# A three-layer CIN kernel: preparation on four array tiles, two blocks by turns at the start, and a tail by quarters

## The chip, the cores and the metric

The kernel runs on one core of a Trainium2 chip. The metric is device time in microseconds (us) of one execution; a median of several runs is given. The profile is one profiled execution, whose span is counted from the first to the last instruction. The engines are called PE (TensorE, the matrix engine), PEld (its weight loads), DVE (VectorE), ACT (ScalarE), POOL (GpSimd) and SP (SyncE). All arithmetic is in fp32.

## The reference

B = 1024 samples have F = 39 fields of E = 64 numbers each. Three layers of a compressed interaction network multiply every feature map with every field and mix the products; each layer is summed over E, and one linear form makes a number of the sums.

```python
def _cin_layer(Xk, X0, W, b):
    O = W.shape[0]
    Hk, Fdim = (Xk.shape[1], X0.shape[1])
    Wr = W.reshape(O, Hk, Fdim)
    return jnp.einsum('bhe,bfe,ohf->boe', Xk, X0, Wr) + b[None, :, None]

X0 = sparse_embedding            # (1024, 39, 64)
Xk = X0
outs = []
for W, b in ((W0, b0), (W1, b1), (W2, b2)):   # (64, 39*39), (64, 64*39), (64, 64*39)
    Xk = _cin_layer(Xk, X0, W, b)
    outs.append(Xk.sum(axis=-1))
cin_output = jnp.concatenate(outs, axis=-1)
return cin_output @ fc_w.T + fc_b             # (1024, 1)
```

The kernels use that all layers but the first are linear in the last feature map. fc's third part times W2 gives a small matrix v2 (64 x 39, with fc's second part as column 40). v2 times W1 gives, for every pair of fields, 64 weights beside the 64 of W0. These 128 weights for each pair of fields (a 41st "field" of ones takes in linear terms) are the table of 1600 rows. Products of fields are formed once for each unordered pair, so that the weights of (a, b) and (b, a) are fetched from the table and added (wa + wb).

## The kernel before

The batch is cut into 32 blocks of 32 samples (2048 columns of sample times E). A block's fields lie in DRAM (xd, two blocks in a table, with a row of ones each). For every block, GpSimd gathers rows into four tiles of 128 partitions, r[n][:, 0..3], so that the six products of two tiles cover nearly all pairs of fields; what is left, half a chunk to a block, is the product of u and v for two blocks at once.

```python
PAIRS = ((0, 1), (0, 2), (0, 3), (1, 2), (2, 3), (1, 3))
NPAIR = len(PAIRS)          # 6
NCHUNK = NPAIR + 1          # 7
MM, SUB, BLK = 512, 1024, 2048
prods = ctx.enter_context(tc.tile_pool(name="prods", bufs=4))
psum = ctx.enter_context(tc.tile_pool(name="psum", bufs=4, space=PSUM))   # tiles of 128 x 1024
...
def gather_rows(dst, n, k):                      # L117
    table = xd[n // 2 % NTAB][: FT if k < 4 else 2 * FT]
    nc.gpsimd.indirect_dma_start(
        dst, None, table, bass.IndirectOffsetOnAxis(ap=lists[:, k : k + 1], axis=0)
    )
def roll(n, tiles=range(4)):
    r[n] = rt[n % 2]
    for i in tiles:
        gather_rows(r[n][:, i], n, n % 2 * 4 + i)
def roll_half(n):
    gather_rows(ut[n // 2 % 2], n, 8)
    gather_rows(vt[n // 2 % 2], n, 9)
```

The preparation loads the weights, forms v2, then the table in DRAM, and fetches the weights of each chunk from it by gathers (cut):

```python
nc.sync.dma_start(w2s, w2.rearrange("o (s n) -> (o s) n", s=2))
for k in range(2):
    nc.scalar.dma_start(fc2[k:128:2, k : k + 1], fcv[:, 2:3])
nc.scalar.dma_start(fc, fcv)
nc.scalar.dma_start(w1s, w1)
load(0, nc.gpsimd)
nc.gpsimd.memset(ones, 1.0)
nc.gpsimd.dma_start(xd[0][F : 2 * FT : FT], ones)
nc.gpsimd.dma_start(tablev[0:F, 0:F, H : 2 * H], w0t)
... # lists of rows, on DVE
roll(0, (0, 1, 2))
for t4 in range(4):                               # v2 = fc . W2
    nc.tensor.matmul(pv[32 * t4 : 32 * t4 + 32, 0:n8], fc2, w2s[:, t4 * n8 : (t4 + 1) * n8], ...)
nc.vector.tensor_copy(vrow, pv[:, 0:n8])
for k in range(2):
    nc.sync.dma_start(v2[32 * k : 32 * k + 32, 0:F], vrow[k:128:32])
...
for g in range(5):                                # v2 . W1, L273
    nc.tensor.matmul(pt[g // 2][at : at + FT, :n], v2, w1v[:, f0:f1, :], start=True, stop=True)
for g in range(5):                                # copies, and into the table
    ...
    engine.dma_start(tablev[:, f0:f1, 0:H], dst.rearrange("b (a h) -> b a h", h=H))
... # ones of the other tables, biases, load(1)
weights(0)
roll(0, (3,))
weights(1)
weights(2)
roll_half(0)
weights(3)
roll(1, (0, 1))
weights(4)
roll(1, (2, 3))
weights(5)
weights(6)
load(2)
load(3)
```

The main loop runs over steps (block, chunk); a product on DVE is four steps ahead of its matmuls, and a block's result is read out after the first step of the next one (cut):

```python
def product(n, c):                                # L324: DVE, 128 x 2048
    i, k = PAIRS[c]
    nc.vector.tensor_tensor(p, r[n][:, i], r[n][:, k], ALU.mult)
def multiply(n, c, p):                            # L341; L352 for the half chunk
    for m in range(BLK // MM):
        nc.tensor.matmul(po[n][m // 2][:, bass.ts(m % 2, MM)], wa[:, c, :], p[:, bass.ts(m, MM)], ...)
def finish(n):
    for h in range(BLK // SUB):                   # L372: ACT, 64 x 1024
        nc.scalar.activation(t, po[n][h][H:128, :], AF.Identity, bias=b0s[H:128])
    for h in range(BLK // SUB):                   # L376, L380: DVE
        nc.vector.scalar_tensor_tensor(gt[0:H], po[n][h][0:H, :], fc[:, 0:1], x1[h], ALU.add, ALU.mult)
        nc.vector.tensor_reduce(sums[:, b_at : b_at + SB], gt.rearrange("p (b e) -> p b e", e=E), AX.X, ALU.add)

steps = []
for n in range(0, NBLK, 2):
    steps += [(n, c) for c in range(NCHUNK)] + [(n + 1, c) for c in range(NPAIR)]
for at, (n, c) in enumerate(steps):
    ...                                           # gathers and loads for later blocks; wa += wb in the first block
    multiply(n, c, p.pop((n, c)))
    if c == 0:
        if n > 0:
            finish(n - 1)
        fields(n)
    if at + AHEAD < len(steps):
        p[steps[at + AHEAD]] = product(*steps[at + AHEAD])
finish(NBLK - 1)
last_weights()
for m in range(B // MM):                          # L427, L428
    nc.tensor.matmul(py[0:1, 0:MM], wfin, sums[:, bass.ts(m, MM)], start=True, stop=True)
    nc.scalar.activation(y[:, bass.ts(m, MM)], py[0:1, 0:MM], AF.Identity, bias=kfin)
nc.sync.dma_start(out.rearrange("b o -> o b"), y)
```

Of the kernel before, what the change touches and what calls it, by code (L numbers as in the profile page):

```python
# [51 lines left out]
F32 = mybir.dt.float32  # L52
I32 = mybir.dt.int32
AF = mybir.ActivationFunctionType
ALU = mybir.AluOpType
# [13 lines left out]
NPAIR = len(PAIRS)  # L69
NCHUNK = NPAIR + 1  # L70
MM = 512
SUB = 1024
BLK = 2048
BB = BLK // E
# [18 lines left out]
def cin_kernel(ctx: ExitStack, tc: tile.TileContext, x, w0t, b0, w1, b1, w2, b2, fc_w, fc_b, out):  # L93
# [7 lines left out]
    psum = ctx.enter_context(tc.tile_pool(name="psum", bufs=4, space=PSUM))  # L101
# [3 lines left out]
    r = {}  # L105
    xd = [dram.tile([2 * FT, BLK], F32, name=f"xd{k}") for k in range(NTAB)]

# [13 lines left out]
    def roll(n, tiles=range(4)):  # L121
        r[n] = rt[n % 2]
        for i in tiles:
            gather_rows(r[n][:, i], n, n % 2 * 4 + i)
# [8 lines left out]
    v2 = const.tile([H, FT], F32, name="v2")  # L133
# [16 lines left out]
    with prep as prep:  # L150
        w2s = prep.tile([128, FH // 2], F32, name="w2s")
        w1s = prep.tile([H, FH], F32, name="w1s")
        fc2 = prep.tile([128, 32], F32, name="fc2")
        ones = prep.tile([2, BLK], F32, name="ones")
        zeros = prep.tile([FT, 2 * H], F32, name="zeros")
# [4 lines left out]
        nc.gpsimd.iota(place, pattern=[[0, 1]], base=0, channel_multiplier=1)  # L160
        nc.vector.memset(fc2, 0.0)
        nc.vector.memset(zeros, 0.0)
        nc.vector.memset(warm, 0.0)
        nc.sync.dma_start(w2s, w2.rearrange("o (s n) -> (o s) n", s=2))
        fcv = fc_w.rearrange("o (l h) -> h (o l)", h=H)
        for k in range(2):
            nc.scalar.dma_start(fc2[k:128:2, k : k + 1], fcv[:, 2:3])
        nc.scalar.dma_start(fc, fcv)
        nc.scalar.dma_start(w1s, w1)
        nc.scalar.copy(warm, warm)  # L170
        load(0, nc.gpsimd)
        nc.gpsimd.memset(ones, 1.0)
        nc.gpsimd.dma_start(xd[0][F : 2 * FT : FT], ones)
        nc.gpsimd.dma_start(tablev[0:F, 0:F, H : 2 * H], w0t)
        nc.gpsimd.dma_start(tablev[:, F, :], zeros)
        nc.gpsimd.dma_start(tablev[F, 0:F, H : 2 * H], zeros[0:F, 0:H])
# [37 lines left out]
        fused(field[0], t, extra, field[0], ALU.mult, ALU.add)  # L214

# [9 lines left out]
        nc.vector.tensor_copy(lists[:, 0:4], fields_of[:, 0:4])  # L225
        nc.vector.tensor_scalar(lists[:, 4:8], fields_of[:, 0:4], float(FT), None, ALU.add)
        nc.vector.tensor_scalar(half, half, float(FT), None, ALU.mult)
        nc.vector.tensor_scalar(lists[:, 8:10], fields_of[:, 4:6], half, None, ALU.add)
        roll(0, (0, 1, 2))


        n8 = 8 * F
        pv = psum.tile([128, SUB], F32, name="pv", tag="po")
        vrow = prep.tile([128, n8], F32, name="vrow")
        for t4 in range(4):
            nc.tensor.matmul(  # L236
                pv[32 * t4 : 32 * t4 + 32, 0:n8],
                fc2,
                w2s[:, t4 * n8 : (t4 + 1) * n8],
                start=True,  # L240
                stop=True,
            )
        nc.vector.tensor_copy(vrow, pv[:, 0:n8])
        nc.vector.tensor_copy(v2[:, F:FT], fc[:, 1:2])
        for k in range(2):
            nc.sync.dma_start(v2[32 * k : 32 * k + 32, 0:F], vrow[k:128:32])
# [20 lines left out]
        part = prep.tile([128, 3, MM], F32, name="part")  # L267
        pt = [psum.tile([128, SUB], F32, name="pt", tag="po") for _ in range(3)]
        for g in range(5):
            f0, f1 = 8 * g, min(8 * g + 8, F)  # L270
            n = (f1 - f0) * H
            at = g % 2 * H
            nc.tensor.matmul(  # L273
                pt[g // 2][at : at + FT, :n], v2, w1v[:, f0:f1, :], start=True, stop=True
            )
        for g in range(5):
            f0, f1 = 8 * g, min(8 * g + 8, F)
            n = (f1 - f0) * H
            at = g % 2 * H
            src, dst = pt[g // 2][at : at + FT, :n], part[at : at + FT, g // 2, :n]  # L280
            if g % 2:
                nc.scalar.copy(dst, src)
            else:
                nc.vector.tensor_copy(dst, src)  # L284
            engine = nc.scalar if g % 2 else nc.sync
            engine.dma_start(tablev[:, f0:f1, 0:H], dst.rearrange("b (a h) -> b a h", h=H))
        for k in range(1, NTAB):
            nc.scalar.dma_start(xd[k][F : 2 * FT : FT], ones)
        for k, t in enumerate((b1, b2)):
            nc.scalar.dma_start(bias[:, k : k + 1], t.rearrange("(h o) -> h o", o=1))  # L290
        nc.scalar.dma_start(b0s[H:128], b0.rearrange("(h o) -> h o", o=1))
        nc.scalar.dma_start(fcb, fc_b.rearrange("(p o) -> p o", o=1))
        load(1)
# [7 lines left out]

    weights(0)
    roll(0, (3,))
    weights(1)
    weights(2)
    roll_half(0)
    weights(3)
    roll(1, (0, 1))
    weights(4)
    roll(1, (2, 3))  # L310
    weights(5)
    weights(6)
    load(2)
# [6 lines left out]
    def product(n, c):  # L320
        p = prods.tile([128, BLK], F32, name="p", tag="p")
        if c < NPAIR:
            i, k = PAIRS[c]
            nc.vector.tensor_tensor(p, r[n][:, i], r[n][:, k], ALU.mult)  # L324
        else:
            nc.vector.tensor_tensor(p, ut[n // 2 % 2], vt[n // 2 % 2], ALU.mult)  # L326
        return p

    def accumulators(n):
        po[n] = [psum.tile([128, SUB], F32, name="po", tag="po") for _ in range(BLK // SUB)]  # L330

    def multiply(n, c, p):
        first = n % 2 == 0
        if c == 0 and first:
            accumulators(n)
        if c == NPAIR:
            accumulators(n + 1)
        for m in range(BLK // MM):
            at = bass.ts(m % 2, MM)
            if c < NPAIR:  # L340
                nc.tensor.matmul(  # L341
                    po[n][m // 2][:, at],
                    wa[:, c, :],
                    p[:, bass.ts(m, MM)],
                    start=(c == 0 and first),
                    stop=(c == NPAIR - 1 and not first),
                )
                continue

            for h in range(2):  # L350
                w = slice(h * HR, (h + 1) * HR)
                nc.tensor.matmul(  # L352
                    po[n + h][m // 2][:, at],
                    wa[w, c, :],
                    p[w, bass.ts(m, MM)],
                    start=(h == 1),
                    stop=(h == 0),
                )
# [9 lines left out]
    def finish(n):  # L368
        x1 = []
        for h in range(BLK // SUB):  # L370
            t = work.tile([H, SUB], F32, name="x1", tag="x1")
            nc.scalar.activation(t, po[n][h][H:128, :], AF.Identity, bias=b0s[H:128])  # L372
            x1.append(t)
        for h in range(BLK // SUB):
            gt = g[n][h]
            nc.vector.scalar_tensor_tensor(  # L376
                gt[0:H], po[n][h][0:H, :], fc[:, 0:1], x1[h], ALU.add, ALU.mult
            )
            b_at = n * BB + h * SB
            nc.vector.tensor_reduce(  # L380
                sums[:, b_at : b_at + SB], gt.rearrange("p (b e) -> p b e", e=E), AX.X, ALU.add
            )

    def last_weights():

        pc = psum.tile([128, SUB], F32, name="pc", tag="po")
        nc.tensor.matmul(pc[0:F, 0:1], v2[:, 0:F], bias[:, 0:1], start=True, stop=True)
        nc.tensor.matmul(pc[0:1, MM : MM + 1], bias[:, 0:1], fc[:, 1:2], start=True, stop=False)
        nc.tensor.matmul(pc[0:1, MM : MM + 1], bias[:, 1:2], fc[:, 2:3], start=False, stop=True)
        nc.vector.memset(wfin[0:H], 1.0)  # L390
        nc.scalar.copy(wfin[H : H + F], pc[0:F, 0:1])
        nc.scalar.activation(kfin, pc[0:1, MM : MM + 1], AF.Identity, bias=fcb, scale=float(E))

    AHEAD = 4
    steps = []
    for n in range(0, NBLK, 2):
        steps += [(n, c) for c in range(NCHUNK)] + [(n + 1, c) for c in range(NPAIR)]
    p = {s: product(*s) for s in steps[:2]}
    for at, (n, c) in enumerate(steps):
        if c == 0:  # L400
            if 0 < n < NBLK - 1:
                roll(n + 1)
                if n % 2:
                    roll_half(n + 1)
            if n + 4 < NBLK:
                load(n + 4)
        if at == 0:
            for k in range(3):
                nc.vector.tensor_tensor(wa[:, k], wa[:, k], wb[:, k], ALU.add)  # L409
                if k < 2:  # L410
                    p[steps[2 + k]] = product(*steps[2 + k])
        elif n == 0 and c + 2 < NCHUNK:
            nc.vector.tensor_tensor(wa[:, c + 2], wa[:, c + 2], wb[:, c + 2], ALU.add)  # L413
        multiply(n, c, p.pop((n, c)))
        if c == 0:
            if n > 0:
                finish(n - 1)
            fields(n)
# [53 lines left out]
```

## Time and profile before

| | us |
|---|---|
| median of 3 runs | 780.49 (777.31 to 780.69) |
| profiled run, its span | 777.1, 775.1 |
| first product matmul starts | 33.3 |
| last product matmul ends | 761.9 |
| VectorE busy | 633.2 (82%) |
| GpSimd busy | 279.2 (36%) |

A line of a group of instructions is read: line of the program, engine, operation, output and input by name, sizes, how many, then busy us and mean ns of one, then the engine's idle time just ahead of them and what ended it. An fp32 matmul leaves two records. The chain of waits follows the work that ended last back to its beginning, so that its pieces add up to the span. A timeline line gives start, duration, engine, line and operation, and in brackets how long the engine was idle before.

### The profile page before, as it was taken

The page shows a single profiled execution, that of the slowest core. Times are in us where ns is not written, and L with a number is a line of the kernel's source. Part 1 is how long each engine was busy: PE and PEld are TensorE (multiplying, and loading weights), DVE is VectorE, ACT ScalarE, POOL GpSimd, SP SyncE. Part 2 cuts the span into 40 slices and gives each one's busy share as a digit, 9 for nine tenths or more (in the row PEclk, how much of TensorE's full clock was granted, in tenths as well). Part 3 has the DMA queues.
Part 4 walks back from the last instruction along what each step waited for, and adds up shares of the span by engine and source line. Part 5 has one row for each costly group of instructions (what it writes and reads, how often), then busy time and mean ns, then how long its engine had stood idle before and what let it go on. Part 6 is the DMA issues. An engine that isn't in the chain of part 4 may idle for free.

```text
span 775.1 us, 4926 instructions
## 1 busy us (share of the span) xinstructions
PE 735.6 (95%) x1820; PEld 316.8 (41%) x1820; DVE 633.2 (82%) x409; ACT 142.2 (18%) x136; POOL 279.2 (36%) x185
## 2 busy tenths in 40 slices
PE   3279999999999999999999999999999999999996
PEld 0134444444444444444444444444444444444442
DVE  4358888889888888988888898888888888889882
ACT  1012212122221212222121222212112221111222
POOL 4487343422334343223434322343432234343000
PEclk9999999999999999999999999999999999999998
DMA  7888875656776565676756567675656757545200
GB/s 202 258 321 318 334 291 217 222 220 233 321 249 276 213 231 213 228 315 249 288 214 224 218 231 301 250 296 219 219 222 227 292 217 309 216 195 214 96 0 0
DMA packets 65480, 181.40 MB, mean 234 GB/s; under 512 B 44345, under 2 KB 44385, under 8 KB 44907
## 3 DMA queue, kind: packets, MB, share of 16 engines
q0 software_dynamic: 23840, 169.46, 56.0%
q1 hardware_dynamic: 40259, 10.79, 6.1%
q10 hardware_dynamic: 1358, 0.84, 0.5%
q8 instruction: 14, 0.23, 0.1%
q14 instruction: 9, 0.07, 0.0%
HBM read 180.58 MB, written 11.10 MB: 247 GB/s over the span
## 4 chain that ended last, share of the span: by engine, by line
PE 92%; DMA 3%; POOL 2%; DVE 2%; issue 1%; ACT 0%; SPq 0%; POOLq 0%; DVEq 0%; ACTq 0%
PE po L341 83%; PE po L352 8%; DMA r<-xd,lists 1%; DMA table<-part 1%; POOL wa L298 1%; DMA v<-vrow 1%; DMA wb<-table,wlists 1%; POOL r L117 1%; PE pt L273 1%; PE py L427 0%; POOL wb L298 0%; DVE g L376 0%; DVE sums L380 0%; DMA bias<-in_b 0%; DVE fields_of L196 0%
## 5 line engine op out<-in xcount | busy, mean ns | idle before, releaser
L341 PE MATMUL po<-p,wa 128*128 128x512 f32 x1536 | 667.8, 596 | 19.3 <-DVE wa L409 15.1
L324 DVE TENSOR_TENSOR p<-r 128x2048 f32<-128x2048 f32 x192 | 435.9, 2291 | 96.9 <-PE po L341 68.3
L341 PEld LDWEIGHTS po<-p,wa 128*128 128x128 f32 x1536 | 291.5, 191 | 395.3 <-issue 383.6
L117 POOL DMA_INDIRECT r<-xd,lists x128 | 211.3, 1651 | 410.5 <-DVE p L324 384.0
L372 ACT ACTIVATE x<-po,b0s 64x1024 f32<-64x1024 f32 x64 | 71.1, 1111 | 427.1 <-PE po L352 244.6
L365 ACT COPY g<-u 39x1024 f32<-39x1024 f32 x64 | 66.6, 1043 | 180.7 <-DVE sums L380 157.2
L376 DVE SCALAR_TENSOR_TENSOR g<-po,fc,x 64x1024 f32<-64x1024 f32 x64 | 81.2, 1269 | 8.7 <-ACT x L372 8.7
L380 DVE TENSOR_REDUCE sums<-g 103x16 f32<-103x1024 f32 x64 | 78.1, 1220 | 2.2
L352 PE MATMUL po<-p,wa 64*128 64x512 f32 x256 | 59.3, 602 | 0.0
L352 PEld LDWEIGHTS po<-p,wa 64*128 64x128 f32 x256 | 23.4, 186 | 34.7 <-issue 34.7
L326 DVE TENSOR_TENSOR p<-u,v 128x2048 f32<-128x2048 f32 x16 | 36.5, 2284 | 0.0
L117 POOL DMA_INDIRECT u<-xd,lists x16 | 28.4, 1772 | 4.9 <-issue 4.9
L117 POOL DMA_INDIRECT v<-xd,lists x16 | 15.0, 940 | 4.9 <-issue 4.6
L298 POOL DMA_INDIRECT wa<-table,wlists x7 | 9.1, 1301 | 13.1 <-DMA bias<-in_b 11.2
L273 PE MATMUL pt<-w1s,v 64*40 64x512 f32 (+1 forms) x10 | 5.6, 1101 | 6.7 <-DMA v<-vrow 6.7
L298 POOL DMA_INDIRECT wb<-table,wlists x7 | 9.4, 1336 | 2.1 <-issue 2.1
L413 DVE TENSOR_TENSOR wa<-wa,wb 128x128 f32<-128x128 f32 x4 | 1.2, 293 | 10.1 <-DMA wb<-table,wlists 10.1
L284 DVE COPY part<-pt 40x512 f32<-40x512 f32 (+1 forms) x3 | 2.0, 661 | 7.3 <-PE pt L273 7.3
L427 PE MATMUL py<-sums,wfin 103*1 103x512 f32 x4 | 3.6, 1049 | 4.3 <-DVE wfin L390 4.3
L236 PE MATMUL pv<-w2s,fc 128*32 128x312 f32 x8 | 1.3, 722 | 5.9 <-DMA fc<-in_fc_w 5.9
L409 DVE TENSOR_TENSOR wa<-wa,wb 128x128 f32<-128x128 f32 x3 | 0.8, 283 | 6.7 <-DMA wb<-table,wlists 6.7
L273 PEld LDWEIGHTS pt<-w1s,v 64*40 64x40 f32 x10 | 1.0, 159 | 10.7 <-issue 10.7
(62 smaller groups left out, 21.9 us busy)
## 6 DMA issues: line engine op xcount, KB each, us to landing
xd<-in_x SPq DMA_DIRECT2D x31, 312.0 KB
r<-xd,lists POOLq DMA_INDIRECT x128, 7.4
w2s<-in_w SPq DMA_DIRECT2D x1, 624.0 KB
w1s<-in_w ACTq DMA_DIRECT2D x1, 624.0 KB
table<-in_w0t POOLq DMA_DIRECT2D x1, 380.2 KB
xd<-in_x POOLq DMA_DIRECT2D x1, 312.0 KB, 7.2
u<-xd,lists POOLq DMA_INDIRECT x16, 8.8
v<-xd,lists POOLq DMA_INDIRECT x16, 9.1
```

Of the source, the lines that this page charges most:

```text
L117: nc.gpsimd.indirect_dma_start(dst, None, table, bass.IndirectOffsetOnAxis(ap=lists[:, k : k + 1], axis=0))
L273: nc.tensor.matmul(pt[g // 2][at : at + FT, :n], v2, w1v[:, f0:f1, :], start=True, stop=True)
L298: nc.gpsimd.indirect_dma_start(w[:, c], None, table[:], bass.IndirectOffsetOnAxis(ap=wlists[:, k, c : c + 1], axis=0))
L324: nc.vector.tensor_tensor(p, r[n][:, i], r[n][:, k], ALU.mult)
L326: nc.vector.tensor_tensor(p, ut[n // 2 % 2], vt[n // 2 % 2], ALU.mult)
L341: nc.tensor.matmul(po[n][m // 2][:, at], wa[:, c, :], p[:, bass.ts(m, MM)], start=(c == 0 and first), stop=(c == NPAIR - 1 and not first),)
L352: nc.tensor.matmul(po[n + h][m // 2][:, at], wa[w, c, :], p[w, bass.ts(m, MM)], start=(h == 1), stop=(h == 0),)
L365: nc.scalar.copy(gt[H : H + F], ut[n // 2 % 2][h : h + F, bass.ts(m, SUB)])
L372: nc.scalar.activation(t, po[n][h][H:128, :], AF.Identity, bias=b0s[H:128])
L376: nc.vector.scalar_tensor_tensor(gt[0:H], po[n][h][0:H, :], fc[:, 0:1], x1[h], ALU.add, ALU.mult)
L380: nc.vector.tensor_reduce(sums[:, b_at : b_at + SB], gt.rearrange("p (b e) -> p b e", e=E), AX.X, ALU.add)
L427: nc.tensor.matmul(py[0:1, 0:MM], wfin, sums[:, bass.ts(m, MM)], start=True, stop=True)
```

## The change

It works on both ends of the program and leaves the middle as it was but for the size of the accumulators.

- Preparation: W1 and W2 are loaded in two halves onto 64 partitions each, so that matmuls of 64 rows run on tiles of the array, four at a time; v2 is turned by VectorE transposes and a copy in place of a DMA through vrow; the table is put together on chip, W0's part too, and written in three transfers of long rows. Idle matmuls on zeros (`spin`) keep TensorE busy.
- Start: the rows of ones come on ScalarE's queue, load(1) early on GpSimd's, and five row gathers go ahead of the weights. The first two blocks take their chunks by turns, three and three, in a new order of chunks, so that fewer weights are needed early.
- Accumulators: eight of one bank (512 columns) in place of four of two.
- End: the last two chunks of the last block are multiplied quarter by quarter, each quarter is read out and summed at once, and the final product is done in three pieces of 512, 504 and 8 columns.

The core of the diff, cut:

```diff
+ORDER = (0, 1, 3, 2, 4, 5)
-    psum = ctx.enter_context(tc.tile_pool(name="psum", bufs=4, space=PSUM))
+    psum = ctx.enter_context(tc.tile_pool(name="psum", bufs=8, space=PSUM))
+    def bank(name):
+        return psum.tile([128, MM], F32, name=name, tag="po")
...
+        load(0, nc.gpsimd)
+        nc.gpsimd.memset(w0s, 0.0)
+        nc.gpsimd.memset(w0r, 0.0)
+        load(1, nc.gpsimd)
...
+        halves(w2s, w2)
+        halves(w1s, w1)
+        nc.scalar.dma_start(fc, fc_w.rearrange("o (l h) -> h (o l)", h=H))
+        load_ones(0, nc.scalar)
+        nc.scalar.copy(warm, warm)
         for k in range(2):
-            nc.scalar.dma_start(fc2[k:128:2, k : k + 1], fcv[:, 2:3])
+            nc.scalar.dma_start(w0s[H * k : H * k + F], w0t[:, NA * k : NA * (k + 1), :])
+        nc.scalar.dma_start(w0r[0:F], w0t[:, 2 * NA : F, :])
+        for s in range(2):
+            nc.scalar.copy(fc2[H * s : H * s + H, 0:1], fc[:, 2:3])
+            nc.scalar.copy(v2[H * s : H * s + H, F:FT], fc[:, 1:2])
...
+        def spin(n):
+            for _ in range(n):
+                nc.tensor.matmul(idle, zeros[:, 0:128], zeros, start=True, stop=True)
+        spin(2)
...
+        roll(0, (0, 1, 2))
+        roll(1, (0, 1))
...
-            nc.sync.dma_start(v2[32 * k : 32 * k + 32, 0:F], vrow[k:128:32])
+            for u in range(4):
+                rows = slice(u % 2 * H, u % 2 * H + H)
+                f0 = u // 2 * 19 + k * 10
+                nc.tensor.matmul(pv[k][32 * u : 32 * u + 32, 0:320], fc2[rows], w2v[rows, f0 : f0 + 10, :], ...)
+        spin(1)
+        ... nc.vector.transpose(blocks[:, 32 * f0 : 32 * (f0 + 10)], pv[k][H * u : H * u + H, 0:320])   # x4
+        nc.vector.tensor_copy(v2[0:H, 0:F], column)
+        nc.scalar.copy(v2[H:128, 0:F], column)
+        nc.scalar.copy(part[:, :, H : 2 * H], w0s.rearrange("b (a h) -> b a h", h=H))
...
+        ... nc.tensor.matmul(pt[s][H * k : H * k + H], v2[rows], w1v[rows, NA * k : NA * (k + 1), :], ...)   # x4
+        ... nc.tensor.matmul(pr[s][rows, 0 : 32 * NR], v2[rows], w1v[rows, 2 * NA : F, :], ...)            # x2
+        spin(9)
+        for s, copy in enumerate((nc.vector.tensor_copy, nc.scalar.copy)):
+            ... copies of pt[s] and pr[s] into part and rest
+        nc.sync.dma_start(tablev[:, 0:NA, :], part[0:FT])
+        nc.scalar.dma_start(tablev[:, NA : 2 * NA, :], part[H : H + FT])
+        nc.sync.dma_start(tablev[:, 2 * NA : FT, :], rest[0:FT])
...
     weights(0)
-    roll(0, (3,))
     weights(1)
+    weights(3)
+    roll(1, (2,))
     weights(2)
-    roll_half(0)
-    weights(3)
-    roll(1, (0, 1))
+    roll(0, (3,))
     weights(4)
-    roll(1, (2, 3))
     weights(5)
+    roll_half(0)
     weights(6)
+    roll(1, (3,))
...
+    steps = [(n, c) for n in range(2) for c in ORDER[:3]]
+    steps += [(0, c) for c in ORDER[3:] + (NPAIR,)] + [(1, c) for c in ORDER[3:]]
+    for n in range(2, NBLK, 2):
+        steps += [(n, c) for c in ORDER + (NPAIR,)] + [(n + 1, c) for c in ORDER]
...
+    last_weights()
+    add(steps[0][1]) ... # first products and adds in turn
+    for at, (n, c) in enumerate(steps[:-TAIL]):
+        add(steps[at + 2][1])
         multiply(n, c, p.pop((n, c)))
+        if at - 1 in over:
+            finish(over[at - 1])
+            fields(over[at - 1] + 1)
         if at + AHEAD < len(steps): ...              # product, and roll(n + 2) after a block's last one
+    for m in range(BLK // MM):
+        for n, c in steps[-TAIL:]:
+            multiply(n, c, p[n, c], (m,))
+        finish_quarter(NBLK - 1, m)                 # ACT 64 x 512, DVE 64 x 512, DVE sum of 103 x 512
+    for lo, hi in ((0, MM), (MM, done), (done, B)):  # done = 1016
+        nc.tensor.matmul(py, wfin, sums[:, lo:hi], start=True, stop=True)
+        if hi < B:
+            nc.scalar.activation(y[:, lo:hi], py, AF.Identity, bias=kfin)
+        else:
+            nc.vector.tensor_scalar(y[:, lo:hi], py, kfin, None, ALU.add)
+    nc.scalar.dma_start(outv[:, 0:done], y[:, 0:done])
+    nc.sync.dma_start(outv[:, done:B], y[:, done:B])
```

## The prediction

> **What bounds the kernel now.** I read the page first, then the chain of waits in order of time, then the timeline of the first 60 us and of the last 15, and last the windows of the start for the DMA rate. The page's groups say what the work is:
>
> ```profile
> span 775.1 us, 4926 instructions
> PE 735.6 (95%) x1820; PEld 316.8 (41%) x1820; DVE 633.2 (82%) x409; ACT 142.2 (18%) x136; POOL 279.2 (36%) x185
> ...
> L341 PE MATMUL po<-p,wa 128*128 128x512 f32 x1536 | 667.8, 596 | 19.3 <-DVE wa L409 15.1
> ```
>
> TensorE is busy 95% of the span, and the 32 blocks x 6 chunks x 4 matmuls stand there as 1536 records, two to an fp32 matmul. The chain of waits gives the rhythm (start, duration, what):
>
> ```profile
> 59.66 0.30 DVE wa L413
> 59.96 0.04 issue
> 60.01 3.70 PE po L341 x8
> 63.71 3.63 PE po L352 x16
> 67.34 41.40 PE po L341 x96
> 108.74 3.63 PE po L352 x16
> 112.37 41.40 PE po L341 x96
> ...
> 742.82 19.09 PE po L341 x44
> 761.91 0.02 issue
> ```
>
> A pair of blocks is 96 records in 41.40 us (0.431 each) and 16 in 3.63, together 45.03 us, fifteen times over without a gap. Sixteen pairs are 16 x 45.03 = 720.5 us that no part of the change shortens. The last matmul ends at 761.9. So everything ahead of the stream, with its stalls, costs 761.9 - 720.5 = 41.4 us (I call it the effective start), and the tail 775.1 - 761.9 = 13.2. Only these 54.6 us are in play.
>
> The effective start is later than the first product matmul, which the timeline puts at 33.3 (start, duration, engine, what; the bracket is the idle time before it):
>
> ```profile
> 12.62 1.03 POOL L117 DMA_INDIRECT r<-xd,lists  x1 [5.14 <-DMA xd<-ones]
> ...
> 27.41 0.95 POOL L298 DMA_INDIRECT wa<-table,wlists  x1 [11.24 <-DMA bias<-in_b]
> 28.66 0.95 POOL L298 DMA_INDIRECT wb<-table,wlists  x1 [0.30 <-issue]
> ...
> 33.32 5.45 PE L341 MATMUL po<-p,wa 128*128 128x512 f32 x8 [13.84 <-DVE wa L409]
> ...
> 39.99 10.57 PE L341 MATMUL po<-p,wa 128*128 128x512 f32 x24 [1.23 <-DVE wa L409]
> ...
> 54.24 5.24 PE L341 MATMUL po<-p,wa 128*128 128x512 f32 x8 [3.68 <-DVE wa L413]
> ```
>
> The table is landed at about 27, the first weights at 32.9; then one block alone eats chunks faster than GpSimd fetches weights, and from 33.3 to 60.0 only 720.5 - 701.9 = 18.6 us of work is done in 26.7. The other 8.1 are gaps and slow records: 8 records in 5.45 us instead of 3.45.
>
> The windows give the DMA rate while row gathers run alone (columns: PE, PEld, DVE, ACT, POOL busy, clock, DMA share, GB/s):
>
> ```profile
> 16.00:18.00 2.00, 2.00 (x5) 0.32 (x2) 0.78 (x2) 0.58 (x1) 0.17 (x1) 1.00 1.03 377
> 18.00:20.00 2.00, 1.48 (x2) 0.00 (x0) 1.07 (x2) 0.58 (x1) 0.00 (x0) 1.00 0.99 365
> 20.00:22.00 2.00, 0.00 (x0) 0.00 (x0) 0.82 (x2) 0.00 (x0) 0.00 (x0) 1.00 1.00 361
> ```
>
> A gather of 128 rows of 8 KB, 1.05 MB, takes 2.8 us at 370 GB/s.
>
> **What the Trainium skill says.** "TensorE: Matmul & The Clock Gate", What's actually happening: the array runs at half rate until it has been busy for about 3.4 us, and falls back after an idle window of that length. The trace agrees: after 13.8 and 3.7 us of idleness four records take 0.85 us each, after 1.2 us none does. A cold start costs 4 x 0.42 = 1.7 us. "DMA: Bandwidth & Descriptors", Queues, rings and completion order: each DMA engine takes one queue in ring order and goes round between queues by packets. GpSimd's q0 has 169.46 MB in 23840 packets, 7.1 KB each; SyncE's loads are 256-byte pieces in another queue. So I expect weights behind row gathers to wait for them, and loads to hold gathers back little. "TensorEngine Tiling (Array Packing)", Key Properties: tiles work independently. The trace has it for two row tiles: 16 half-row records in 3.63 us against 8 full ones in 3.45. Four tiles are not shown in it. "GPSIMD Engine Reference", Specifications: GpSimd shares its SBUF interfaces with VectorE. The trace agrees: an issue of a gather takes 0.94 us, and up to 2.5 when a product runs.
>
> **The change part by part.**
>
> 1. fc·W2 without a round trip. Now vrow goes through a DMA: from 7.75 (issue) to the first W1 matmul at 13.87 it is 6.1 us. After: fc has to land (issue at 0.95 on ScalarE's queue; now, issued third, it ends its issue at 2.86 and lands by 8.98; I take 7), ScalarE copies columns (four of about 0.2, the third being the one that counts: 8.0), two rounds of four tiles with 320 columns (0.72 a record for 312 now, two records a matmul: 2 x 2 x 0.72 = 2.9, to 10.9), then the last two of four VectorE transposes at about 0.4 each and a column copy of 0.2: v2 at about 12.0. Small gain, 1.8 us.
> 2. W1 on four tiles: now 5.6 us for ten records at about 0.56 apart. After: one round of 512 columns (two records of 1.1) and one of 224 (two of 0.5) = 3.2 us, to 15.2. Copies of 0.7 and about 0.4, most of it beside the matmuls: 15.9.
> 3. The table is written as 40 runs of 8 KB in three transfers instead of 256-byte pieces, for the most part, in eight. The wait on it is 18.6 to 25.5 now, and two bias loads push the first weight fetch to 27.4. After, with the biases gone from this place, I give it 5 us beside running gathers: table at about 21.
> 4. Gathers start earlier and are five instead of three. Now the first waits until 12.6 for the row of ones, which went through GpSimd's queue. After, the ones go from ScalarE's queue, and load(0) sets the start: its issue ends at 2.64 and its landing takes 7.2, so about 10.2. Issues of 0.95 + 0.30 end at 16.4. The fifth is needed for block 1 but stands in the queue before the first weights: data from about 11.7, 5 x 2.8 = 14.1, plus about 2 for table writes, load(1) and loads between: 27.8. wa and wb of the first chunk (0.13 MB) come directly behind, and with about 1.2 until VectorE sees them, its add starts at 29.0. The first matmul at 29.3: 4.0 us before the present 33.3.
> 5. Two blocks by turns: the first three chunks serve six steps. A step is 8 x 0.431 = 3.45 us; a chunk needs two weight issues, 2.5 us undisturbed, and the present sequence of 21 issues took 32.3 us, 1.54 each. From 21 on the 19 issues that are left (14 of weights, 5 of rows) take 29 and are over by about 50; the last, r1's tile 3, lands by 54 and its product is done by 57. The half step's weights are added behind that product in VectorE's order, and the half step is the tenth: 31.0 + 9 x 3.45 = 62. It has 5 us to spare, so the 8.1 us of gaps fall away, except for a cold start.
> 6. The spins: nine zero matmuls, 18 records. From 15.2 they last 7.8 us warm, to about 23, or 24.7 if they start cold. With the first product at 29.3 the gap is 4 to 6 us, longer than the 3.7 that was cold: I charge 1.7. Effective start 29.3 + 1.7 = 31.0, against 41.4: gain 10.4.
> 7. The middle: eight one-bank accumulators hold the same 8 x 512 columns as four of two banks. Four evictions of 64x512 replace two of 64x1024 (1.11 on ScalarE, 1.27 on VectorE) and add about 0.1 each. VectorE has 38.9 busy of 45 us in a pair, ScalarE 8.6. No change: 720.5.
> 8. The tail by quarters. Now the last matmul is followed by 1.12 + 1.29 + 1.22 + 1.20 + 1.22 of halves, 3.59 of the final matmuls at half rate, 0.68 of ScalarE and 2.6 to the end of the output transfer. After: ScalarE 64x512 0.6 (a 40x512 copy takes 0.58), VectorE 0.7 and a sum of 0.65, the last 8 columns 0.3 (a one-column matmul takes 0.18), VectorE 0.15, transfer 2.6, steps between 0.3: 5.3. The other 1016 columns are multiplied under this. A quarter's two steps take 1.72 us on TensorE and about 1.35 on VectorE, so earlier quarters do not pile up. Gain 7.9.
>
> Sum: span 31.0 + 720.5 + 5.3 = 756.8, which is 18.3 less. Timed runs before: 777.3 to 780.7, the profiled one 777.1 for a span of 775.1. Adding 2 to 5.4 to 756.8 gives 758.8 to 762.2; I take 760.5.
>
> **The rivals.** (a) The DMA engines become the bound of the start. All of loads 2 to 5 are issued by SyncE right behind the table; if they share evenly with the gathers (about 1.4 us of all engines each: q1's 6.1% of the span for 31 loads and little else), the first weights land at 33 instead of 29, and the time is 764 to 766. For it: DMA share 0.9 to 1.0 from 2 to 10 us and from 16 to 24. Against it: 361 to 377 GB/s between 16 and 22. (b) The table is the bound, and the gathers ahead of it are quicker than I think: fetch at 21, first product at 25.5, spins still warm; effective start 26, time 755. (c) A new wait in the first pair: VectorE holds the add of the half chunk behind a product that waits for the last gather, or an issue is slowed to 2.5 us each by products. Nineteen issues at 2.3 end at 65, the add comes at about 71, and the wait costs 9 us: time 770. The mean of 1.54 under much the same products speaks against it. (d) The middle gets stalls from the smaller evictions: 0.2 us a block would be 6 us. The 6 us of idle VectorE in a pair speak against it.
>
> **Range and chances.** The tail is sure to about 1.5 us, the start to about 5, the difference between runs is 3. That gives 752 to 768 for 8 in 10. Faster by over 2% means below 764.9: 0.80. Rival (a) or part of (c) leads to within 2%: 0.18. Slower by over 2%: 0.02.
>
> **What would show it.** The chain of waits after should show pieces of 45.03 us from the third block on; the first product matmul at 28 to 30 with eight slow records or fewer; no gap above 1 us in the thirteen first steps; and less than 6 us behind the last matmul. First-weight fetches issued by 22 but added only at 29 would prove the queue (4) and not the table (3) to be the bound. If the stream starts at 33 or shows gaps before the half step, (a) or (c) is right and I am wrong; if pairs take more than 45.1 us, (d).

## The result and the profile after

The changed kernel takes 768.2 us (767.1 to 768.8), beside 780.6 for the kernel before in the same rounds. The ratio is 0.985, with a 95% interval of 0.982 to 0.988. That is 1.5% less time, where 2.6% was predicted; the time lies 0.2 us above the range. The span is 766.5 where 756.8 was predicted, 9.7 more. The time is off by only 7.7, because the prediction added 3.7 us to its span and the executions take 1.8 more than their spans; that it came so near is luck.

The page of the changed kernel, its head and the costliest group:

```profile
span 766.5 us, 5146 instructions
PE 745.1 (97%) x1856; PEld 322.3 (42%) x1856; DVE 641.2 (84%) x479; ACT 160.4 (21%) x207; POOL 320.4 (42%) x185
L391 PE MATMUL po<-p,wa 128*128 128x512 f32 (+1 forms) x1792 | 724.3, 597 | 11.9 <-DVE wa L471 11.9
```

TensorE's idle time ahead of these matmuls fell from 19.3 to 11.9 us, but 6.0 of the 7.4 lie ahead of the first of them (13.84 before, 7.85 now), where idle matmuls now fill the time. All that is left are waits for an add of weights (L471), and most of the expected gain at the start did not come. The timeline shows where (start, duration, engine, line, operation; in brackets the idle time before):

```profile
17.49 0.27 SPq L344 DMA_DIRECT2D table<-rest  x1
28.36 0.95 POOL L351 DMA_INDIRECT wa<-table,wlists  x1 [12.75 <-DMA table<-rest]
33.13 29.25 PE L391 MATMUL po<-p,wa 128*128 128x512 f32 x64 [7.85 <-DVE wa L471]
55.70 0.94 POOL L122 DMA_INDIRECT v<-xd,lists  x1 [0.30 <-issue]
63.89 2.29 DVE L379 TENSOR_TENSOR p<-u,v 128x2048 f32<-128x2048 f32 x1 [9.12 <-DMA v<-xd,lists]
66.10 0.28 DVE L471 TENSOR_TENSOR wa<-wa,wb 128x128 f32<-128x128 f32 x1
66.44 13.95 PE L391 MATMUL po<-p,wa 128*128 128x512 f32 x35 [4.06 <-DVE wa L471]
```

Two things are to be seen. The last table transfer is issued at 17.5, but the first weight fetch, which waits for it, comes at 28.4, and so the first product matmul at 33.1, no earlier than before (33.3). It also comes after 7.85 us of idleness, and 64 records take 29.25 us where 64 x 0.431 = 27.6 would do: 1.7 lost to a cold start (the granted clock is 0.50 from 33 to 36). Then the ninth step waits 4.06 us. VectorE adds its weights only after the product of u and v, which stands ahead in its order and waits 9.1 us for v, issued by GpSimd at 55.7. That gap brings a second cold start (clock 0.50 from 68 to 70).

The chain of waits names the same three holders, and then runs to the end on TensorE (start, duration, what):

```profile
17.49 10.15 DMA table<-rest
...
53.30 7.05 DMA u<-xd,lists
...
66.10 0.30 DVE wa L471
66.44 695.02 PE po L391 x1728
...
761.48 0.69 ACT x1q L429
762.20 0.75 DVE g L430
762.98 0.70 DVE sums L432
763.81 0.21 PE py L506 x2
```

The last block's read-out after the last matmul is one chain of 0.69 + 0.75 + 0.70, and eight columns of the final product follow. The windows of the middle show TensorE full, as before (columns: PE, PEld, DVE, ACT, POOL busy, clock, DMA share, GB/s):

```profile
105.00:150.00 45.00, 45.00 (x113) 19.62 (x112) 39.44 (x26) 9.64 (x12) 22.43 (x12) 1.00 0.70 257
```

The weight loads of the half chunk come at 106.50 and 151.53, one pair of blocks or 45.03 us apart; fourteen such pairs lead to 736.94.

To sum this up I first have to mend the split that the prediction made of the kernel before. Its timeline has

```profile
742.75 20.87 PE L341 MATMUL po<-p,wa 128*128 128x512 f32 x48
...
768.26 3.57 PE L427 MATMUL py<-sums,wfin 103*1 103x512 f32 x4 [4.32 <-DVE wfin L390]
```

so its last matmul ends at 763.6. The chain of waits leaves TensorE at 761.9, because the read-out of the first half begins under the last four records. (So the gaps and slow records between 33.3 and 60.0 were 9.8 us, not 8.1.) With 720.5 us for sixteen pairs, the two ends are:

| | before | after | gain | predicted gain |
|---|---|---|---|---|
| effective start (end of last matmul - 720.5) | 43.1 | 41.0 | 2.1 | 10.4 |
| behind the last matmul | 11.5 | 5.0 | 6.5 | 7.9 |
| span | 775.1 | 766.5 | 8.6 | 18.3 |

With this split the prediction stood for 12.1 us less at the start (43.1 to 31.0) and 6.2 less behind the last matmul (11.5 to 5.3). The second came, of the first 2.1. The 41.0 are 33.13 for the first matmul, 1.66 and about 1.7 for two cold starts, 4.06 for the gap, and some 0.4 of small gaps; the prediction's 31.0 were 29.3 and one cold start of 1.7.

### The profile page after: what moved, and what is told of

Same layout as the page of the kernel before. It is cut to its first block, busy times and chain, and to the rows that moved or that the text cites. A ratio compares the mean times of both kernels' runs of the same rounds, so it can differ in the third digit from the quotient of the medians.

```text
span 766.5 us, 5146 instructions
## 1 busy us (share of the span) xinstructions
PE 745.1 (97%) x1856; PEld 322.3 (42%) x1856; DVE 641.2 (84%) x479; ACT 160.4 (21%) x207; POOL 320.4 (42%) x185
## 4 chain that ended last, share of the span: by engine, by line
PE 91%; DMA 3%; issue 2%; POOL 2%; DVE 1%; ACT 0%; DVEq 0%; POOLq 0%; SPq 0%
PE po L391 91%; DMA table<-rest 1%; POOL wa L351 1%; DMA u<-xd,lists 1%; POOL wb L351 1%; DMA wb<-table,wlists 0%; PE pt L322 0%; DVE blocks L289 0%; POOL r L122 0%; DVE fields_of L233 0%; DVE tmp L229 0%; DVE tmp L233 0%; PE pr L331 0%; DVE g L430 0%; DVE sums L432 0%
## 5 line engine op out<-in xcount | busy, mean ns | idle before, releaser
L391 PE MATMUL po<-p,wa 128*128 128x512 f32 (+1 forms) x1792 | 724.3, 597 | 11.9 <-DVE wa L471 11.9
L391 PEld LDWEIGHTS po<-p,wa 128*128 128x128 f32 (+1 forms) x1792 | 315.0, 190 | 420.4 <-issue 395.4
L122 POOL DMA_INDIRECT r<-xd,lists x128 | 249.3, 1948 | 366.0 <-DVE p L377 340.0
L410 ACT ACTIVATE x<-po,b0s 64x512 f32<-64x512 f32 x124 | 84.5, 684 | 356.4 <-PE po L391 349.8
L416 DVE SCALAR_TENSOR_TENSOR g<-po,fc,x 64x512 f32<-64x512 f32 x124 | 86.4, 734 | 0.0
L351 POOL DMA_INDIRECT wa<-table,wlists x7 | 11.0, 1573 | 14.6 <-DMA table<-rest 12.8
L211 PE MATMUL idle<-zeros 128*128 128x512 f32 x24 | 12.9, 686 | 1.5 <-DVE fc L171 1.5
L471 DVE TENSOR_TENSOR wa<-wa,wb 128x128 f32<-128x128 f32 x7 | 2.0, 291 | 11.6 <-DMA wb<-table,wlists 11.6
L211 PEld LDWEIGHTS idle<-zeros 128*128 128x128 f32 x24 | 4.8, 212 | 8.2 <-issue 6.8
L430 DVE SCALAR_TENSOR_TENSOR g<-po,fc,x1q 64x512 f32<-64x512 f32 x4 | 3.0, 742 | 5.3 <-ACT x1q L429 5.3
L278 PE MATMUL pv<-w2s,fc 64*32 64x320 f32 x16 | 2.8, 764 | 4.5 <-ACT fc L199 4.5
L429 ACT ACTIVATE x1q<-po,b0s 64x512 f32<-64x512 f32 x4 | 2.7, 684 | 10.2 <-PE po L391 10.2
```

What stands on the lines that cost most here:

```text
L122: nc.gpsimd.indirect_dma_start(dst, None, table, bass.IndirectOffsetOnAxis(ap=lists[:, k : k + 1], axis=0))
L211: nc.tensor.matmul(idle, zeros[:, 0:128], zeros, start=True, stop=True)
L278: nc.tensor.matmul(pv[k][32 * u : 32 * u + 32, 0:320], fc2[rows], w2v[rows, f0 : f0 + 10, :], start=True, stop=True,)
L351: nc.gpsimd.indirect_dma_start(w[:, c], None, table[:], bass.IndirectOffsetOnAxis(ap=wlists[:, k, c : c + 1], axis=0))
L391: nc.tensor.matmul(po[n + h][m], wa[w, c, :], p[w, bass.ts(m, MM)], start=c == opens[n + h], stop=c == closes[n + h],)
L410: nc.scalar.activation(x1[m // 2][:, bass.ts(m % 2, MM)], po[n][m][H:128], AF.Identity, bias=b0s[H:128])
```

## The experiments

The theory: the start is held by the time that the table's own transfers take to land, and then by the order in which VectorE adds weights behind products that wait for gathers; the tail's gain is as predicted. The rivals: the five row gathers hold the table; the loads of later blocks hold the table or the weights; the cold start is the loss. Ratios are against runs of the kernel before on the same chip and have a 95% interval; times inside are those of each kernel's profile.

**Fewer gathers ahead of the table.** Two of the five go behind the first weights.

```diff
         roll(0, (0, 1, 2))
-        roll(1, (0, 1))
...
     weights(1)
+    roll(1, (0, 1))
     weights(3)
```

> The changed kernel, but only the three row gathers of block 0 go ahead of the table; the two of block 1 come after the weights of the first two chunks. Queue theory: the table's transfers are held by the row gathers that stand in another queue, so without two of them the table lands at about 22 us instead of 28, and the first product matmul starts at about 27 instead of 33. GpSimd then has two more issues between the table and u and v, at 1.8 us each, so the stream's stall ends some 3 us earlier at best: span about 763. Rival: the table's transfers take their 10 us by themselves (long rows written to DRAM), then the table lands at 28 as before, two issues are added behind it, and the span is about 770.

Measured: the fetch moved from 28.36 to 26.13, 8.8 us after the last table issue instead of 10.9; the first matmul to 32.05. Ratio 0.986 (0.982 to 0.990), the same as the change. Two gathers hold the table by about 2 us, not by the 5.6 which they themselves take, and the ninth step, whose weights are added behind the product of u and v, starts only 0.9 earlier, so nothing is left of it.

**No gathers ahead of the table.** All five go behind the first weights; one run, for the profile alone.

> The changed kernel with no row gather ahead of the table (block 0's three come after the weights of the first chunk, block 1's two after those of the second). A look at the table's own time only; the span is of no interest and will be longer. With three gathers ahead it landed at 26.1 us although the gathers were through by 20; from 22 to 24 the DMA share was 0.65 at 165 GB/s. Theory: the table's three transfers from 40 partitions run on part of the DMA engines, some ten of 16, at about 16 GB/s each: 0.82 MB in about 5 us and 2 us of latency, so the table lands at about 24.5 even with an empty queue. Rival: contention with the gathers is all; then it lands at about 21.

The timeline of that kernel:

```profile
18.86 0.27 SPq L342 DMA_DIRECT2D table<-rest  x1
27.36 1.03 POOL L349 DMA_INDIRECT wa<-table,wlists  x1 [22.16 <-DMA xd<-in_x]
```

and one of its windows between them:

```profile
20.00:22.00 2.00, 2.00 (x6) 0.93 (x5) 0.00 (x0) 0.00 (x0) 0.00 (x0) 1.00 0.63 161
```

With no row gather in the queues the fetch still comes 8.5 us after the last table issue (8.2 after its end), and meanwhile the DMA engines move 161 GB/s, where in the same two microseconds of the changed kernel, with the gathers, they move 420. So the larger part of the delay is there without any gather; by these single profiles, three of them ahead add 0.3 us to the 8.5 and five add 2.4. In this kernel's trace the table's packets run from 19.1 to 26.2, so only the last 1.2 us lie between the data and the fetch. Loads of later blocks share the queues in that time. The bracket names another transfer as the last of those awaited; it is that of a wait on several (in the same kernel with 48 rows, below, it names the table). Row products come too late here: first matmul 45.3, 774.7 us.

**A table of 48 rows.** The part that is written gets 48 rows, of which 40 are used (39 fields and the row of ones). The Trainium skill, "DMA: Bandwidth & Descriptors", Why a DMA increments its semaphore by 16 and not by 1, says that a DMA runs on the largest number of engines up to 16 that divides the slowest dimension of both its sides: by that ten for 40 rows, sixteen for 48.

```diff
+    TR = 48
-    table = dram.tile([FT * FT, 2 * H], F32, name="table")
+    table = dram.tile([TR * FT, 2 * H], F32, name="table")
-        nc.sync.dma_start(tablev[:, 0:NA, :], part[0:FT])
+        nc.sync.dma_start(tablev[:, 0:NA, :], part[0:TR])      # the other two likewise
```

> The changed kernel with a table of 48 rows of fields instead of 40 (eight are zero and never read), so that each of the three transfers comes from 48 partitions and 0.98 MB are written instead of 0.82. If 40 partitions use only ten DMA engines and 48 use 16, each engine writes 61 KB instead of 82 KB, and the table lands at about 26 us instead of 28.4, with the first product matmul at 31; span about 764 to 765. Rival: all engines take part already, or the writes wait for the gathers anyway: then 20% more bytes land at 28.5 or later, and the span stays at 766.5 or grows by 1.

Measured: issue 17.40, fetch 26.72, 1.6 us earlier after it than in the change; but the first matmul at 32.98. Ratio 0.988 (0.985 to 0.991): no gain. Done without gathers ahead as well (one run):

> No row gather ahead of the table, and a table of 48 rows of fields: a look at the table's own time. With 40 rows it took 8.2 us from the last issue (18.9) to the first fetch (27.1) with nothing else in the queues but one load and the rows of ones. If ten of 16 engines were the reason, 48 rows on 16 engines take 6 to 6.5 us for 20% more bytes. If bytes or the writes' latency set it, 8 to 9.5 us.

Issue 18.17, fetch 25.76: 7.3 us after the end of the issue, against 8.2 with 40 rows. More rows help by 0.9 though they write a fifth more; sixteen engines for ten would make 8.2 into some 6.2 (an estimate: 8.2 x 10/16 x 1.2) if their number were all. The runs agree with the page in direction and no further.

**Loads held back.** A transfer of one number that reads the weights of the fourth chunk stands ahead of load(2) on SyncE's queue, so that loads 2 to 5 wait for it.

```diff
+    hold = dram.tile([1, 1], F32, name="hold")
+    nc.sync.dma_start(hold, wb[0:1, 3, 0:1])
     load(2)
     load(3)
```

> The changed kernel, with SyncE's loads of the blocks from the third on held back by one tiny transfer that waits for the third chunk's weights (about 40 us). In the changed kernel these loads of 256-byte pieces follow the table directly, and from 29 to 34 us the DMA share is 0.9 to 1.0 at only 205 GB/s while the first weights are on their way: 3.1 us from issue to the add, after a table that took 10. Theory: without the loads the first product matmul starts at about 31 instead of 33.1 and u and v land about 2 us earlier; span 764. Rival: the loads take only time that nobody needs; first matmul at 33, span 766.5 within 0.7, or more where the later loads collide with u and v.

```profile
18.00 0.27 SPq L344 DMA_DIRECT2D table<-rest  x1
29.00 0.95 POOL L351 DMA_INDIRECT wa<-table,wlists  x1 [13.45 <-DMA table<-rest]
```

Measured: from the last table issue to the fetch 11.0 us, where the change takes 10.9. So with five gathers ahead, the loads behind the table do not hold it. The first matmul comes at 33.14, and the ratio is 0.987 (0.984 to 0.990): as the change. Windows around the first weights, of the changed kernel and then of this one:

```profile
30.00:32.00 2.00, 0.00 (x0) 0.00 (x0) 0.00 (x0) 0.00 (x0) 1.51 (x2) 0.50 0.94 209
```

```profile
30.00:32.00 2.00, 0.00 (x0) 0.00 (x0) 0.00 (x0) 0.00 (x0) 1.44 (x2) 0.50 0.19 47
```

The DMA engines are nearly empty now (0.19 for 0.94), and the first matmul moves little: it comes 15.1 us after the last table issue instead of 15.6. A full DMA row in a window is no proof that the transfer one waits for is held by it. Between the fetch and the add stand two issues of 0.95 with 0.3 between in both kernels, and then 2.1 us of landing in the change and 1.5 here.

**More spins.** `spin(9)` becomes `spin(18)`, so that the array is warm for the first product.

> The changed kernel with 18 idle matmuls instead of nine, so that TensorE is busy until about 32.7 us, shortly before the first product matmul at 33.1. The first four records should take 0.43 us instead of 0.85. If the start of the stream sets the end, the span falls by 1.7 us to 764.8. My theory: no gain, 766.5 within 0.7, since the ninth step waits for u and v's gather anyway, and the gap before it grows from 4.1 to 5.8 us.

The timeline of that kernel:

```profile
34.70 20.84 PE L391 MATMUL po<-p,wa 128*128 128x512 f32 x48 [1.19 <-DVE wa L471]
...
67.92 10.42 PE L391 MATMUL po<-p,wa 128*128 128x512 f32 x27 [5.04 <-DVE wa L471]
```

After 1.19 us of idleness 48 records take 0.434 each, so the cold start is gone. The gap ahead of the ninth step has grown from 4.06 to 5.04, since u and v set when that step begins: whatever the eight steps before it gain is waited for again. Ratio 0.988 (0.986 to 0.991).

**Weights added one step earlier.** The add of a step's weights stands ahead of the product of u and v in VectorE's order.

```diff
-        add(steps[at + 2][1])
+        add(steps[min(at + 3, len(steps) - 1)][1])
```

> The changed kernel, but VectorE adds the weights of a step ahead of the next step's product instead of behind it. Theory: the 4.06 us gap before the ninth step comes from the add of its weights standing behind the product of u and v, which waits for a gather; the weights themselves had landed long before. Then the ninth step starts at 62.4 without a gap, the cold restart (1.7 us) goes, and the next step starts at about 66.6, when the product of u and v is done: span 761.5, 5 us less. Rival: the weights of that chunk came late themselves; then the gap stays and the span stays at 766.5.

The timeline of that kernel:

```profile
33.89 33.32 PE L391 MATMUL po<-p,wa 128*128 128x512 f32 x72 [7.79 <-DVE wa L471]
65.11 2.29 DVE L379 TENSOR_TENSOR p<-u,v 128x2048 f32<-128x2048 f32 x1 [9.11 <-DMA v<-xd,lists]
...
71.97 24.50 PE L391 MATMUL po<-p,wa 128*128 128x512 f32 x56 [0.60 <-DVE p L377]
97.63 12.68 PE L391 MATMUL po<-p,wa 128*128 128x512 f32 x36 [1.16 <-DVE p L377]
```

Nine steps (72 records) now run without a gap, though v comes as late as before: the order was what turned its wait into one of TensorE's. Ratio 0.982 (0.979 to 0.985), which is 0.003 below the change's: 2.3 us with an uncertainty of 3. In the profiles the last product matmul ends at 759.65 for 761.46, though the first starts 0.76 later; so 2.6 us came of the 4.06 + 1.7 that the gap costs. That the order made the gap is shown, and what moving the add is worth in time is not clear of the noise. Part is handed on: VectorE has stood idle for 9.11 us behind v, and TensorE waits later, 0.46 us at 67.7 for an add, then 0.60 and 1.16 for products.

**The tail as it was.** The last block is multiplied and read out whole, with two final matmuls of 512 columns and one output transfer; the one-bank accumulators stay.

```diff
-    for m in range(BLK // MM):
-        for n, c in steps[-TAIL:]:
-            multiply(n, c, p[n, c], (m,))
-        finish_quarter(NBLK - 1, m)
+    finish(NBLK - 1)
-    for lo, hi in ((0, MM), (MM, done), (done, B)):
+    for lo, hi in ((0, MM), (MM, B)):
-    nc.scalar.dma_start(outv[:, 0:done], y[:, 0:done])
-    nc.sync.dma_start(outv[:, done:B], y[:, done:B])
+    nc.sync.dma_start(outv, y)
```

> The changed kernel with the end as before: the last block read out only when all of it is multiplied, two final products of 512 columns and one output transfer. If the tail by quarters carries the whole gain, the span grows from 766.5 to 772 or 773 (0.7 + 5.4 of read-outs and sums, 1.7 for one final product at half rate, 0.7, 2.6, so 11 us behind the last matmul instead of 5.0), still a little less than the 13.2 before, since the final weights and the first of the two final products are early now. Rival: the gain is from the start, and the span stays within 1 us of 766.5.

The timeline of its end:

```profile
744.63 14.32 PE L391 MATMUL po<-p,wa 128*128 128x512 f32 x33
...
761.33 1.22 DVE L421 TENSOR_REDUCE sums<-g 103x16 f32<-103x1024 f32 x1
762.70 1.02 PE L503 MATMUL py<-sums,wfin 103*1 103x512 f32 x2 [2.79 <-DVE sums L421]
```

Its last product matmul ends at 758.95 (earlier than in the change, as the gap ahead of the ninth step was 2.26 in this run) and its span is 766.8, so 7.85 us lie behind it: 2.85 more than with quarters. The mean of four spans is 769.1, also 2.8 more than that of the change, taken in other rounds; the ratio, 0.991 (0.989 to 0.994), is 0.006 above the change's, 5 us with an uncertainty of 3. The other 3.65 us of the tail's gain are not the quarters'. From the end of the last sum to the output's issue, the kernel before takes 768.11 to 772.58 = 4.5 us, and this one 762.55 to 764.46 = 1.9. In the kernel before both final matmuls wait until 768.26 for the clearing of wfin, which stands behind the read-outs in VectorE's order, and then run at half rate, four records in 3.57. With the final weights made early, the first of them is done under the read-out, and two records take 1.02. That is 2.6 of the 3.65; the rest is not taken apart.

**Versions put together.** Four runs join what the others showed. All add the weights one step earlier, put ScalarE's copies of fc ahead of its loads of W0 (the table's last issue comes at 14.6 to 15.6 instead of 17.5), and issue u and v before the weights of the last chunks. The first also takes the chunks of the two blocks strictly by turns, with four gathers ahead and 13 spins:

```diff
-    steps = [(n, c) for n in range(2) for c in ORDER[:3]]
+    steps = [(n, c) for c in ORDER[:3] for n in range(2)]
```

> The changed kernel with four edits at the start: blocks 0 and 1 alternate chunk by chunk for six steps (each chunk's weights serve two steps running), four row gathers instead of five ahead of the table and u and v ahead of the weights of the last three chunks, weights added ahead of the next step's product, and ScalarE's copies of fc ahead of its loads of W0, with 13 idle matmuls. Theory: GpSimd's issues, not the weights' number alone, set the first pair; in this order every gather lands before its product is due. First matmul at 30 to 31, warm, gaps below 1 us in the first thirteen steps: effective start 31 to 33, span 757 to 759. Rival: some gather is late all the same and a gap of 3 us or more with a cold restart stays: span 762 to 765.

Fetch 26.03, first matmul 31.22, ratio 0.985 (0.983 to 0.986); a gap of 2.25 us stays at 70.9. The second has 48 rows on top:

> The same with the table of 48 rows of fields. If the wider table lands 2 us earlier, and the table sets the first matmul, then 2 us less than with 40: span 755 to 757. If the gathers hold it anyway, the same as with 40 within 1 us.

Fetch 25.27, but first matmul 32.92, as the issue of the second fetch takes 2.93 instead of 0.95 beside a product; ratio 0.983 (0.981 to 0.985). The third adds the held loads and 17 spins:

> The alternating order with the table of 48 rows, plus the held loads, and 17 idle matmuls instead of 13 so that TensorE stays warm. That order's last run had its first matmul at 32.9, cold, and an effective start of 35.8. If loads and cold clock are what is left: first matmul at 30 to 31, warm, gaps of 1 us: effective start 31 to 32, span 757 to 758. Rival: the rows of the blocks' third tiles are still late for the third and fourth step: span 760 to 761 as without the two edits.

Fetch 25.41, first matmul 30.64 and warm; ratio 0.983 (0.980 to 0.986). The windows from 28 to 30 us, first of the change with 48 rows alone and then of this kernel, show how full the DMA engines were while the first weights came:

```profile
28.00:30.00 2.00, 0.00 (x0) 0.00 (x0) 0.00 (x0) 0.00 (x0) 1.70 (x2) 1.00 1.04 268
```

```profile
28.00:30.00 2.00, 0.78 (x8) 0.28 (x6) 2.00 (x1) 0.40 (x2) 1.70 (x2) 1.00 0.42 102
```

Full engines in the first, with 6.3 us from the fetch at 26.72 to the first matmul; 0.42 in the second, with 5.2. Holding the loads may be worth something once the table comes early. The second kernel also has a gather less ahead, so this is a reading and not a measurement of it. The fourth goes back to the change's order of steps and its five gathers:

> The same edits, but with the change's own order of steps (three chunks of block 0, then three of block 1) and its five gathers ahead of the table; u and v before the weights of the last three chunks. If the order of steps matters less than the loads, the order of adds and the clock, the same span as with alternation within 1.5 us (757 to 760). If it matters, since the fifth gather stands ahead of the table and each chunk's weights serve one step before the next is due, 2 to 4 us more: 760 to 762.

It keeps the 48 rows, the held loads and the 17 spins. Its timeline:

```profile
31.89 61.99 PE L394 MATMUL po<-p,wa 128*128 128x512 f32 x144 [3.30 <-DVE wa L474]
94.21 1.98 PE L394 MATMUL po<-p,wa 128*128 128x512 f32 x4 [0.33 <-DVE p L380]
```

144 records without a gap of note, in 61.99 us, and the next wait is 0.33. The table's last issue comes at 14.71, 2.7 us earlier than with 48 rows alone, but the fetch at 25.95 only 0.8 earlier: behind five gathers the table takes 11.2 us even with 48 rows and no loads in its queue. Its landing is no fixed time after its issue. Its last product matmul ends at 756.2, an effective start of 35.7. Median 763.0 (762.4 to 764.0), ratio 0.981 (0.979 to 0.983): the fastest of all that ran, below the change with held loads of the same session (0.984 to 0.990) without overlap, and not to be told from the kernel with the add order alone (0.979 to 0.985). All four stayed behind the spans of 755 to 760 that their theories gave: their mean spans are 763.5, 762.1, 762.5 and 761.1.

## Why the prediction was off, point by point

- **Parts 1 and 2**, slightly off: v2 came at 14.0 for 12.0 and the W1 matmuls ended at 17.0 for 15.2. The copies of fc stand behind three loads in ScalarE's order and came at 9.53, not 8.0, and the W2 matmuls at 9.8. fc was not late: where the copies stand first (the first of the versions put together), they run from 4.88. The issue of the table was thus 1.6 later than the 15.9 assumed.
- **Part 3 is the step that failed first.** "I give it 5 us beside running gathers" was 10.9 from the last issue to the fetch. About 8.5 of that remains with no gather ahead; some 2 are the gathers'. The 5 was not worked out: the prediction's own line had 6.9 us (18.6 to 25.5) for the table of short rows, and that long rows would be quicker was assumed.
- **Part 4**: its test was stated, first fetches issued by 22 and added at 29 if the queue were the bound. The fetch came at 28.4 and the add at 32.7, so the table was the bound. The gathers started at 9.55; the 10.2 assumed would have been 9.8 by the prediction's own 2.64 + 7.2. The queue may be a second one behind it, as the kernels with 48 rows suggest. The gain of 4.0 us at the first matmul was 0.2.
- **Part 5 failed too, and separately.** The half step's weights were said to have "5 us to spare" behind the product waiting for the last gather. It was the ninth step's add, behind the product of u and v, and it had none: v is GpSimd's sixteenth issue after the table; the fifteen ahead of it began at 28.4 instead of 21 and took 1.82 us each instead of 1.54, so that it went out at 55.7 and its product was done at 66.2. Rival (c) had the mechanism, with other tiles and 9 us for it; it cost 5.8 with the cold start. Moving the add by one step removed the gap, so the order is shown to be its cause.
- **Part 6**: one cold start was charged and two came, 1.7 each. Avoiding the first was worth nothing while the gap behind it was there.
- **Part 7 held**: 45.03 us a pair.
- **Part 8 held**: 5.0 behind the last matmul for 5.3. The gain is 6.5 and not 7.9 only because 1.7 us of the old tail were still matmuls. What earns it was told incompletely: 2.85 are the quarters', and 3.65 remain without them, which I put down to the earlier final weights and the one-bank read-outs.
- **Rivals (a), (b), (d)**: (d) fell. (b), with a quick table, fell. (a) named loads as the bound of the start: with the loads held the first matmul stays where it was, so they weren't, in this kernel. (The DMA share read as 0.9 to 1.0 from 2 to 10 us is 0.82 from 2 to 4.) The sign that was named for (a) or (c), a stream that starts at 33, came from the table, which neither names. The size of (a) (764 to 766) was nearer than mine for another reason.

What stays open is why the table takes 8 us for 0.82 MB with no gather ahead. The time from its last packet to GpSimd's issue is only 1.2 of it. Its write from few rows and the loads that follow are not told apart there: the loads were held only behind five gathers, where they made no difference.

## What to carry to other kernels

Where a small table goes out to memory and is fetched again, take the round trip from a transfer of that kind in a profile, not from the rate of large gathers; all that is planned behind it hangs on this one number. Before trusting that a wait has time to spare, list what stands ahead of it in the same engine's order: an add of 0.3 us behind a product that waits for a gather inherits the gather's whole delay, and one place forward in the order took a gap of 4.06 us away. When a fix takes one wait away, look for the next one close behind: fewer gathers, more rows, held loads and more spins each did what they were made for, and none alone moved the time.

## What was not expected of the hardware

- From the end of the last of three issues that write 0.82 MB from 40 rows to the fetch that waits for them were 8.2 us with no row gather queued, and 7.3 with 48 rows. All queues together moved 105 to 217 GB/s in windows of 2 us then, against 356 to 420 in the change from 16 to 24 us, with gathers queued.
- Two row gathers, 2.1 MB, that were queued ahead of the table cost it only about 2 us, less than the 5.6 that they take alone at 370 GB/s.
- The W1 matmuls read their 512 columns with a stride and took 8 records on four tiles in 2.17 us, 1.1 for one record at a granted clock of 1.00, against 0.43 for one with columns side by side.
